# Routing stage of a convolution, mixture-of-experts and attention kernel: one product for centred channels and logits, choices marked on GpSimd, keys in one pass

## The chip, the cores and the metric

The kernel runs on one core of one Trainium2 chip. The metric is the time of one execution on the device in microseconds. The kernel before was run ten times: median 9578.8 us, from 9575.91 to 9595.06.

A core has five engines that this document names as the profile does: PE (matrix products; PEld is its weight load), DVE (vector operations), ACT (activation functions and scaled copies), POOL (GpSimd; it also issues the indirect transfers) and SP (issues most plain transfers). Each takes its own instructions in the order in which they were built and waits for the others by semaphores.

## The reference, cut to what matters

The input `x` is 32 images of 128 channels, 56 x 56. A layer of convolution with a mixture of experts is followed by a layer of attention with a second mixture; all is float32. The change lies in the routing of the first layer. There are T = 100352 tokens (one for each pixel), C = 128 channels, E = 8 experts, two choices a token:

```python
x = conv(input, dw_kernel) + dw_bias            # depthwise 7 x 7
mu = x.mean(-1); var = x.var(-1)
x = (x - mu) / sqrt(var + 1e-06) * ln_gamma + ln_beta
logits = x @ Wg + bg
topv, topi = top_k(logits, 2)
wts = softmax(topv)
order = argsort(-wts[:, 0])                     # tokens by their first weight
cap = int(1.25 * T / E)                         # places of an expert, filled in this order
```

A choice counts only while its expert has a place left. The kept tokens go through the experts and their weighted results come back to the tokens.

## The kernel before, in words

The kernel runs in stages, one after the other, over tiles of 128 partitions:

- **Convolution** (to about 700 us): 128 channels, one after the other; the result goes to `conv_d` in memory.
- **Route** (L323 to L393): the tokens in NG = 112 groups of 896, a group being GJ = 7 tiles of 128 tokens. `route(g)` is a generator whose `yield`s mark its steps; `in_turn` (L179) takes one step of each group under way in turn, so that several groups interleave. The scheduler then fixes the order on each engine.
- **Selection** (L397 to L654): for each expert, the tokens' keys, and by 24 halvings the threshold above which tokens are kept.
- **Scatter** (L659 to L808): group by group, the places of the kept tokens are worked out and their rows sent to the experts' buffer `xb_d` by indirect transfers.
- **Experts**, **attention** (from L926) and the **second mixture and output** follow; the change does not touch them.

`route(g)` in steps, with its lines:

1. L358: SP loads the group's channels into `ct` (four buffers, from pool `rt`).
2. L364: PE multiplies each of the seven tiles by `jm` (128 wide), which gives the centred channels (with the sign turned) in PSUM tiles `pc` of four tiles' width, four buffers of one bank. ACT squares them: four tiles singly with a running sum (L372), three in one go (L367), whose sums DVE makes (L368). L377: PE multiplies the same seven tiles by the 8 columns of `rw` that hold the routing weights; the logits before scaling are in `pl`, two buffers. A float32 product is two instructions of PE in the trace.
3. `inverse` (L139): ACT makes mean square plus eps, logarithm and exponential (L143 to L145), then POOL makes one Newton step in four operations (L147 to L150). The result is 1/sqrt(var), in `rst`.
4. DVE scales the logits by it (L381) and adds their constant part `cb` (L382); they are in `lgs`.
5. DVE finds the eight largest of each tile's logits (L387, seven MAX8) and their indices (L389, seven FIND_INDEX8, each with a load of values). ACT copies the first two of both into `pk` (L390, L391), a tile of four numbers a token.

After all groups, the selection begins at L405: from the two largest logits come `ex`, `den`, `share` and the priority `prio` (L405 to L413). Then for each expert e the key (L417 to L423): two DVE passes compare the two index columns of `pk` with e, a third multiplies by `prio`, and ACT subtracts a constant. One pass is over 784 numbers in each of 128 partitions.

In the scatter, `places(g)` (L749) writes a group's seven row numbers a partition into `rd`, which has the pool's four buffers; `send(g)` (L796) issues seven indirect transfers on POOL from them (L697). The rows themselves are in six tiles `xs`.

Of the kernel before, what the change touches and what calls it, by code (L numbers as in the profile page):

```python
# [8 lines left out]
F32 = mybir.dt.float32  # L9
I32 = mybir.dt.int32  # L10
U32 = mybir.dt.uint32
AF = mybir.ActivationFunctionType
ALU = mybir.AluOpType
AX = mybir.AxisListType
# [3 lines left out]
P = 128  # L18
GJ = 7
# [6 lines left out]
def conv_attn_hybrid_kernel(  # L26
# [24 lines left out]
    nc = tc.nc  # L51
    N, C, H, W = x.shape
    HW = H * W
    T = N * HW
    E = Wg.shape[1]
# [19 lines left out]
    TC = T // P  # L75
# [43 lines left out]
    def over(t, n):  # L119
        return t.unsqueeze(2).to_broadcast([t.shape[0], t.shape[1], n])  # L120

    def across(t, n):
        return t.unsqueeze(1).to_broadcast([t.shape[0], n, t.shape[1]])
# [12 lines left out]
    def by_tile(t):  # L136
        return t.rearrange("c (j p) -> c j p", p=P)
# [61 lines left out]
    with tc.tile_pool(name="cv_c", bufs=1) as cc, tc.tile_pool(  # L199
        name="cv", bufs=3  # L200
# [20 lines left out]
        for c in range(C):  # L221
# [15 lines left out]
            for kw in range(KS):  # L237
                for r in range(2):
                    rows = slice(r * HP, r * HP + H)
                    for b in range(2):  # L240
# [4 lines left out]
                            start=(kw == 0),  # L245
                            stop=(kw == KS - 1),
# [18 lines left out]
    CHUNKS = ((0, 4), (4, GJ))  # L265
# [5 lines left out]
    rst = ch.tile([P, TC], F32, name="rst")  # L271
# [38 lines left out]
    count = ch.tile([P, P // E], F32, name="count")  # L310
# [7 lines left out]
    rw = ch.tile([C, RO], F32, name="rw")  # L318
    cb = ch.tile([P, C + E], F32, name="cb")

    pairs = ExitStack()
    pk = pairs.enter_context(tc.tile_pool(name="pairs", bufs=1)).tile([P, TC, 4], F32, name="pk")
    with tc.tile_pool(name="rt_c", bufs=1) as cc, tc.tile_pool(  # L323
        name="rt", bufs=4
    ) as rt, tc.tile_pool(name="rt_p", bufs=2, space=PSUM) as rtp:
        tc.keep_in_program_order(
            nc.scalar.preload_act_table_set("natural_log_exp_and_others")
        )
        gam = cc.tile([C, 1], F32, name="gam")
        nc.sync.dma_start(gam, ln_gamma.unsqueeze(1))  # L330
        nc.sync.dma_start(bet, ln_beta.unsqueeze(1))
        wg = cc.tile([C, E], F32, name="wg")
        nc.sync.dma_start(wg, Wg)
        bgt = cc.tile([P, E], F32, name="bgt")
        nc.sync.dma_start(bgt, bg.partition_broadcast(P))

        jm = cc.tile([C, C], F32, name="jm")
        nc.vector.tensor_scalar(jm, ident, 1.0 / C, None, ALU.subtract)
        raw = cc.tile([C, RO], F32, name="raw")
        nc.vector.tensor_copy(raw[:, :C], ident)  # L340
        nc.vector.tensor_copy(raw[:, C : C + C], turn)
        nc.vector.tensor_copy(raw[:, C + C :], wg)

        ps = rtp.tile([P, RO], F32, name="pa", bufs=1)
        nc.tensor.matmul(ps, bet.to_broadcast([C, P]), raw, start=True, stop=True)
        nc.vector.tensor_copy(cb[:, :C], ps[:, :C])
        nc.vector.tensor_tensor(cb[:, C:], ps[:, C + C :], bgt, ALU.add)
        nc.vector.tensor_scalar(raw, raw, gam, None, ALU.mult)
        ps = rtp.tile([P, RO], F32, name="pa", bufs=1)
        nc.tensor.matmul(ps, jm, raw, start=True, stop=True)  # L350
        nc.vector.tensor_copy(rw, ps)

        def route(g):
            pr, gl = divmod(g, GPP)
            cols = slice(g * GJ, (g + 1) * GJ)
            ct = rt.tile([C, GT], F32, name="ct")
            for im, px, col, n in segments(gl):
                nc.sync.dma_start(ct[:, col : col + n], conv_d[2 * pr + im, :, px : px + n])  # L358
            yield
            ss = rt.tile([P, GJ], F32, name="ss")  # L360
            for i, (j0, j1) in enumerate(CHUNKS):
                ps = rtp.tile([P, 4, C], F32, name="pc", bufs=4)
                for j in range(j0, j1):
                    nc.tensor.matmul(ps[:, j - j0, :], by_tile(ct)[:, j, :], jm, start=True, stop=True)  # L364
                if i:
                    sq = rt.tile([P, GJ - 4, C], F32, name="sqs", bufs=2)
                    nc.scalar.activation(sq, ps[:, : j1 - j0, :], AF.Square)  # L367
                    nc.vector.tensor_reduce(ss[:, j0:j1], sq, AX.X, ALU.add)  # L368
                else:
                    for j in range(j0, j1):  # L370
                        sq = rt.tile([P, C], F32, name="sq", bufs=2)
                        nc.scalar.activation(  # L372
                            sq, ps[:, j - j0, :], AF.Square, accum_out=ss[:, j : j + 1]
                        )
            pl = rtp.tile([P, GJ, E], F32, name="pl")
            for j in range(GJ):
                nc.tensor.matmul(pl[:, j, :], by_tile(ct)[:, j, :], rw[:, C + C :], start=True, stop=True)  # L377
            yield
            yield from inverse(rt, ss, 0, "rst", 3, rst[:, cols])
            lg = lgs[:, cols, :]  # L380
            nc.vector.tensor_tensor(lg, pl, over(rst[:, cols], E), ALU.mult)  # L381
            nc.vector.tensor_tensor(lg, lg, across(cb[:, C:], GJ), ALU.add)  # L382
            yield
            m8 = rt.tile([P, GJ, 8], F32, name="m8")
            i8 = rt.tile([P, GJ, 8], U32, name="i8")
            for j in range(GJ):
                nc.vector.max(m8[:, j, :], lg[:, j, :])  # L387
            for j in range(GJ):
                nc.vector.max_index(i8[:, j, :], m8[:, j, :], lg[:, j, :])  # L389
            nc.scalar.copy(pk[:, cols, 0:2], m8[:, :, 0:2])  # L390
            nc.scalar.copy(pk[:, cols, 2:4], i8[:, :, 0:2])  # L391

        in_turn(route(g) for g in range(NG))  # L393

    with tc.tile_pool(name="sel", bufs=1) as se, tc.tile_pool(  # L397
        name="sel2", bufs=2
# [1 line left out]


        HALF = 2.0**23
        ea = [pk[:, :, 2], pk[:, :, 3]]
        ex = se.tile([P, TC], F32, name="ex")
        nc.vector.tensor_tensor(ex, pk[:, :, 1], pk[:, :, 0], ALU.subtract)  # L405
        nc.scalar.activation(ex, ex, AF.Exp)
# [4 lines left out]
        prio = se.tile([P, TC], F32, name="prio")  # L411
# [3 lines left out]
        nc.vector.memset(less, -HALF)  # L415
        key = se.tile([P, E, TC], F32, name="key")
        for e in range(E):  # L417
            nc.vector.tensor_scalar(key[:, e, :], ea[0], float(e), None, ALU.is_equal)
            nc.vector.scalar_tensor_tensor(
                key[:, e, :], ea[1], float(e), key[:, e, :], ALU.is_equal, ALU.add  # L420
            )
            nc.vector.tensor_tensor(key[:, e, :], key[:, e, :], prio, ALU.mult)
            nc.scalar.activation(key[:, e, :], key[:, e, :], AF.Identity, bias=less)  # L423

        def total(cnt):
# [233 lines left out]
    with tc.tile_pool(name="sc_c", bufs=1) as cc, tc.tile_pool(  # L659
        name="sc", bufs=4  # L660
# [88 lines left out]
        def places(g):  # L749

            of = ofs.pop(g)
            ve.tensor_tensor(of, of, nexts.pop(g), ALU.mult)
            at_ = sc.tile([P, GJ], F32, name="at", bufs=2)
            ve.tensor_reduce(at_, of, AX.X, ALU.add)
            rds[g] = sc.tile([P, GJ], I32, name="rd")
            ve.tensor_scalar(rds[g], at_, float(ROWS), None, ALU.add)

        def add_beta(g):
# [772 lines left out]
```

## Time and profile before

| | us |
|---|---|
| median of 10 runs | 9578.8 |
| lowest and highest | 9575.91 and 9595.06 |
| the profiled execution | 9579.57 |
| its span | 9577.9 |

Busy time in its span, and in the stages as the table of windows gives them:

| window, us | what runs there | PE | DVE | ACT | POOL | granted clock |
|---|---|---|---|---|---|---|
| whole span | | 8677.5 | 6478.3 | 5266.4 | 6773.6 | 0.942 |
| 0 to 700 | convolution | 684.15 | 132.28 | 83.56 | 3.73 | 1.00 |
| 700 to 1063 | route | 356.69 | 274.65 | 247.28 | 94.45 | 0.98 |
| 1063 to 1098 | keys | 0.00 | 34.66 | 9.27 | 3.39 | 0.50 |
| 1098 to 1315 | thresholds, sizes | 57.81 | 169.33 | 110.78 | 19.03 | 0.60 |
| 1315 to 2340 | scatter | 786.94 | 832.06 | 374.26 | 775.22 | 0.93 |
| 2340 to 4430 | experts | 1950.50 | 494.70 | 712.93 | 1623.97 | 0.98 |
| 4430 to 9000 | attention | 4325.30 | 4376.55 | 3712.33 | 4253.83 | 0.98 |
| 9000 to 9578 | second mixture, output | 516.14 | 164.12 | 15.97 | 0.00 | 0.57 |

How to read it: the stages follow each other, so the engine that bounds one of them is seen only in its own row. The granted clock is the share of full speed at which PE may run. A group of instructions is printed as line, engine, operation, tiles written and read, sizes, count, then busy us, mean ns of one, and the idle time before them with what ended it. A tile's name stands without its buffer number, and a line of a helper stands for all that call it (L161 is that of the class which keeps an order of the text).

### The profile page before, as it was taken

What the parts mean: (1) busy time and instruction counts of PE and PEld (TensorE: products, weight loads), DVE (VectorE), ACT (ScalarE), POOL (GpSimd) and SP (SyncE); (2) the same over time, 40 slices, a digit from 0 to 9 for tenths busy, and PEclk for the clock granted to TensorE, in tenths of its full rate; (3) what the DMA queues carried; (4) which work ended last, traced back from release to release, by engine and by line L of the source; (5) the groups of instructions that cost most, each with busy time, mean ns of one, the idle gap of its engine ahead of it and who ended that gap; (6) DMA issues with size and microseconds to landing.
All of it is one profiled execution on the core that took longest, in us unless ns stands there. A gap on an engine that the chain in (4) does not pass through costs nothing. (4 is left out here: it accounts for less than half of the span.)

```text
span 9577.9 us, 165805 instructions
## 1 busy us (share of the span) xinstructions
PE 8677.5 (91%) x62536; PEld 7131.6 (74%) x62536; DVE 6478.3 (68%) x10965; ACT 5266.4 (55%) x13385; POOL 6773.6 (71%) x4884
## 2 busy tenths in 40 slices
PE   9999467776999999997999999999999999999888
PEld 3569445555766666666888998998988898889853
DVE  2127888885222222226999999999999999999423
ACT  1117633333333333335888888888888888888400
POOL 0002147776777777787999999999999999999300
PEclk9999789998999999999999999999999999999765
DMA  9995247775444444441000000000000000000389
GB/s 209 213 200 147 59 124 211 209 207 157 70 70 63 65 68 70 69 69 32 24 31 31 31 31 30 25 27 31 31 31 31 31 24 31 31 31 26 98 279 331
DMA packets 1019570, 849.94 MB, mean 89 GB/s; under 512 B 525876, under 2 KB 912247, under 8 KB 999250
## 3 DMA queue, kind: packets, MB, share of 16 engines
q1 hardware_dynamic: 464018, 479.57, 18.0%
q0 software_dynamic: 177664, 188.81, 11.2%
q10 hardware_dynamic: 377088, 170.96, 6.7%
q8 instruction: 495, 8.11, 0.4%
q14 instruction: 305, 2.50, 0.1%
HBM read 486.34 MB, written 353.64 MB: 88 GB/s over the span
## 5 line engine op out<-in xcount | busy, mean ns | idle before, releaser
L161 POOL TENSOR_TENSOR s<-s,q 128x2048 f32<-128x2048 f32 x784 | 3597.5, 4599 | 137.8 <-DVE s L161 104.5
L161 ACT ACTIVATE s<-s 128x2048 f32<-128x2048 f32 x784 | 1500.6, 1914 | 686.3 <-POOL s L161 683.6
L161 POOL DMA_INDIRECT t_d<-ys,xe x992 | 1530.5, 1543 | 417.1 <-issue 229.9
L161 DVE TENSOR_TENSOR s<-kv,c 128x2048 f32<-128x2048 f32 x784 | 1788.4, 2281 | 7.9 <-POOL c L161 7.6
L161 DVE TENSOR_TENSOR ev<-s,kv 128x2048 f32<-128x2048 f32 x784 | 1785.7, 2278 | 2.3 <-ACT s L161 2.2
L161 PE MATMUL sm<-ident,ev 128*128 128x128 f32 x12544 | 1532.5, 276 | 45.9 <-DVE ev L161 45.9
L161 PE MATMUL sm<-ident,s 128*128 128x128 f32 x12544 | 1524.9, 275 | 8.0 <-ACT s L161 8.0
L161 PEld LDWEIGHTS sm<-ident,ev 128*128 128x128 f32 x12544 | 1437.6, 144 | 93.6 <-DVE ev L161 51.3
L161 PEld LDWEIGHTS sm<-ident,s 128*128 128x128 f32 x12544 | 1402.9, 143 | 20.5 <-ACT s L161 8.4
L888 ACT ACTIVATE hT<-ph,b1t 128x512 f32<-128x512 f32 (+1 forms) x992 | 679.6, 685 | 1239.5 <-PE ph L884 1224.0
L899 DVE TENSOR_TENSOR ys<-py,b2t 128x512 f32<-128x512 f32 (+1 forms) x248 | 171.5, 691 | 1536.1 <-PE py L894 1439.3
L894 PEld LDWEIGHTS py<-w,hT 128*128 128x128 f32 x7936 | 961.1, 193 | 202.5 <-issue 92.2
L884 PE MATMUL ph<-xeT,w 128*128 128x512 f32 (+1 forms) x1984 | 923.3, 598 | 70.6 <-DVE xeT L880 70.6
L894 PE MATMUL py<-w,hT 128*128 128x128 f32 x7936 | 985.1, 278 | 0.2
L697 POOL DMA_INDIRECT xb_d<-xs,rd x784 | 766.6, 978 | 240.2 <-issue 199.2
L241 PE MATMUL cps<-xin,br 56*64 56x448 f32 x7168 | 684.2, 539 | 12.8 <-DVE br L235 10.6
L884 PEld LDWEIGHTS ph<-xeT,w 128*128 128x128 f32 x1984 | 348.7, 191 | 393.8 <-issue 294.1
L161 PE MATMUL pa<-rw,ct 128*128 128x256 f32 x1568 | 422.5, 414 | 203.2 <-DVE xs L161 203.2
L241 PEld LDWEIGHTS cps<-xin,br 56*64 56x64 f32 x7168 | 345.2, 132 | 350.9 <-issue 310.7
L161 PEld LDWEIGHTS pa<-rw,ct 128*128 128x128 f32 x1568 | 299.8, 203 | 335.8 <-DVE xs L161 248.0
L287 POOL MEMSET code<- 128x64 f32 x1 | 0.2, 152 | 693.2 <-DMA conv_d<-ot 693.2
L161 PE MATMUL kv<-wq,zT 128*128 128x256 f32 x1568 | 416.8, 389 | 54.6 <-DVE ev L161 54.2
(327 smaller groups left out, 13452.3 us busy)
## 6 DMA issues: line engine op xcount, KB each, us to landing
ct<-conv_d SPq DMA_DIRECT2D x192, 448.0 KB
xin<-in_x_dram SPq DMA_DIRECT2D x256, 196.0 KB
conv_d<-ot ACTq DMA_DIRECT2D x512, 98.0 KB
t_d<-xs ACTq DMA_DIRECT2D x112, 448.0 KB
tr<-t_d SPq DMA_DIRECT2D x112, 448.0 KB
to<-t_d SPq DMA_DIRECT2D x32, 1568.0 KB
out_dram<-oo ACTq DMA_DIRECT2D x32, 1568.0 KB
xg<-in_x_dram SPq DMA_DIRECT2D x96, 448.0 KB
```

Source lines behind the costliest of these rows:

```text
L161: r = getattr(self.engine, name)(*a, **k)
L241: nc.tensor.matmul(pss[r][b * HP : (b + 1) * HP], br[rows, kw, :], xi[rows, b * NB : (b + 1) * NB, kw : kw + W], start=(kw == 0), stop=(kw ...
L287: nc.gpsimd.memset(code, -1.0)
L697: s = nc.gpsimd.indirect_dma_start(out=xb_d, out_offset=bass.IndirectOffsetOnAxis(ap=idx, axis=0), in_=row, in_offset=None, bounds_check=R ...
L884: nc.tensor.matmul(ph[:, :, :rows], w1[:, f * P : (f + 1) * P], xT[:, :, :rows], start=True, stop=True,)
L888: nc.scalar.activation(hT[:, f, :, :rows], ph[:, :, :rows], AF.Gelu, bias=b1t[:, f : f + 1])
L894: nc.tensor.matmul(py[:rows, j, :], hT[:, f, j, :rows], w2[:, f, :], start=(f == 0), stop=(f == NF - 1),)
L899: nc.vector.tensor_tensor(ys[:rows], py[:rows], across(b2t, SB)[:rows], ALU.add)
```

## The change

Route:

- `jl` holds `jm` and the 8 columns of the routing weights side by side, 136 columns, and one product a tile gives both the centred channels and the logits. The seven tiles of a group lie in PSUM as `pc`, two banks with three tiles each and two buffers, and `po`, one tile, two buffers.
- Of the squares, tiles 0 to 2 and 6 are taken singly and tiles 3 to 5 in one go.
- The logits are scaled from `pc` in one DVE operation of six tiles and from `po` in a second. The constant part is added by POOL instead of DVE.
- The two largest logits are copied to `pk`, now two numbers a token; the two indices go to `ei`. POOL subtracts both from the numbers 0 to 7 (`off`), and the product of the two differences, zero for the two experts that were chosen, is in `hot`.

Selection: a key is one DVE pass, `hot` equal to zero times `prio`, and the same ACT operation behind it.

Scatter: `rd` has eight buffers in place of four.

```diff
-    pk = pairs.enter_context(tc.tile_pool(name="pairs", bufs=1)).tile([P, TC, 4], F32, name="pk")
+    pa_ = pairs.enter_context(tc.tile_pool(name="pairs", bufs=1))
+    pk = pa_.tile([P, TC, 2], F32, name="pk")
+    hot = pa_.tile([P, TC, E], F32, name="hot")
...
+        CE = C + E
+        jl = cc.tile([C, CE], F32, name="jl")
+        nc.vector.tensor_copy(jl[:, :C], jm)
+        nc.vector.tensor_copy(jl[:, C:], rw[:, C + C :])
+        JH = GJ // 2
...
-            for i, (j0, j1) in enumerate(CHUNKS):
-                ps = rtp.tile([P, 4, C], F32, name="pc", bufs=4)
-                for j in range(j0, j1):
-                    nc.tensor.matmul(ps[:, j - j0, :], by_tile(ct)[:, j, :], jm, start=True, stop=True)
-                if i:
-                    sq = rt.tile([P, GJ - 4, C], F32, name="sqs", bufs=2)
-                    nc.scalar.activation(sq, ps[:, : j1 - j0, :], AF.Square)
-                    nc.vector.tensor_reduce(ss[:, j0:j1], sq, AX.X, ALU.add)
...
-            pl = rtp.tile([P, GJ, E], F32, name="pl")
+            pc = rtp.tile([P, 2, 512], F32, name="pc")
+            po = rtp.tile([P, CE], F32, name="po")
+            at_ = pc[:, :, : JH * CE].rearrange("p i (j c) -> p i j c", c=CE)
             for j in range(GJ):
-                nc.tensor.matmul(pl[:, j, :], by_tile(ct)[:, j, :], rw[:, C + C :], start=True, stop=True)
+                nc.tensor.matmul(
+                    po if j == 2 * JH else at_[:, j // JH, j % JH, :], by_tile(ct)[:, j, :], jl,
+                    start=True, stop=True,
+                )
+            for j in (*range(JH), 2 * JH):
+                sq = rt.tile([P, C], F32, name="sq", bufs=2)
+                nc.scalar.activation(
+                    sq, po[:, :C] if j == 2 * JH else at_[:, 0, j, :C], AF.Square,
+                    accum_out=ss[:, j : j + 1],
+                )
+            sq = rt.tile([P, JH, C], F32, name="sqs", bufs=2)
+            nc.scalar.activation(sq, at_[:, 1, :, :C], AF.Square)
+            nc.vector.tensor_reduce(ss[:, JH : 2 * JH], sq, AX.X, ALU.add)
...
-            nc.vector.tensor_tensor(lg, pl, over(rst[:, cols], E), ALU.mult)
-            nc.vector.tensor_tensor(lg, lg, across(cb[:, C:], GJ), ALU.add)
+            r = rst[:, cols]
+            nc.vector.tensor_tensor(
+                lg[:, : 2 * JH].rearrange("p (i j) e -> p i j e", i=2), at_[:, :, :, C:],
+                r[:, : 2 * JH].rearrange("p (i j) -> p i j", i=2).unsqueeze(3).to_broadcast(
+                    [P, 2, JH, E]
+                ),
+                ALU.mult,
+            )
+            nc.vector.tensor_scalar(lg[:, 2 * JH], po[:, C:], r[:, 2 * JH :], None, ALU.mult)
+            nc.gpsimd.tensor_tensor(lg, lg, across(cb[:, C:], GJ), ALU.add)
...
-            nc.scalar.copy(pk[:, cols, 0:2], m8[:, :, 0:2])
-            nc.scalar.copy(pk[:, cols, 2:4], i8[:, :, 0:2])
+            nc.scalar.copy(pk[:, cols, :], m8[:, :, 0:2])
+            ei = rt.tile([P, GJ, 2], F32, name="ei")
+            nc.scalar.copy(ei, i8[:, :, 0:2])
+            yield
+            off = rt.tile([P, 2, GJ, E], F32, name="off_")
+            nc.gpsimd.tensor_tensor(
+                off, count[:, :E].unsqueeze(1).unsqueeze(1).to_broadcast([P, 2, GJ, E]),
+                ei.rearrange("p j i -> p i j").unsqueeze(3).to_broadcast([P, 2, GJ, E]),
+                ALU.subtract,
+            )
+            nc.gpsimd.tensor_tensor(hot[:, cols, :], off[:, 0], off[:, 1], ALU.mult)
...
-            nc.vector.tensor_scalar(key[:, e, :], ea[0], float(e), None, ALU.is_equal)
             nc.vector.scalar_tensor_tensor(
-                key[:, e, :], ea[1], float(e), key[:, e, :], ALU.is_equal, ALU.add
-            )
-            nc.vector.tensor_tensor(key[:, e, :], key[:, e, :], prio, ALU.mult)
+                key[:, e, :], hot[:, :, e], 0.0, prio, ALU.is_equal, ALU.mult
+            )
...
-            rds[g] = sc.tile([P, GJ], I32, name="rd")
+            rds[g] = sc.tile([P, GJ], I32, name="rd", bufs=8)
```

In the changed kernel the product is L374, the squares L380 and L385, the sums L386, the scaling L391 and L398, POOL's add L399, MAX8 and FIND_INDEX8 L404 and L406, the copies L407 and L409, `off` L412, `hot` L417, `ex` L430 and the key's pass L443.

More of the change, by code (lines that the diff above doesn't have):

```diff
@@ L351, in conv_attn_hybrid_kernel @@
         nc.vector.tensor_copy(rw, ps)
+        CE = C + E
[3 more added lines that the diff above has]
+        JH = GJ // 2
+        assert 2 * JH + 1 == GJ and JH * CE <= 512
         def route(g):
@@ L360, in route @@
             ss = rt.tile([P, GJ], F32, name="ss")
-            for i, (j0, j1) in enumerate(CHUNKS):
-                ps = rtp.tile([P, 4, C], F32, name="pc", bufs=4)
-                for j in range(j0, j1):
-                    nc.tensor.matmul(ps[:, j - j0, :], by_tile(ct)[:, j, :], jm, start=True, stop=True)
-                if i:
-                    sq = rt.tile([P, GJ - 4, C], F32, name="sqs", bufs=2)
-                    nc.scalar.activation(sq, ps[:, : j1 - j0, :], AF.Square)
-                    nc.vector.tensor_reduce(ss[:, j0:j1], sq, AX.X, ALU.add)
[L369 to L373, printed above, removed]
-                        )
-            pl = rtp.tile([P, GJ, E], F32, name="pl")
-            for j in range(GJ):
-                nc.tensor.matmul(pl[:, j, :], by_tile(ct)[:, j, :], rw[:, C + C :], start=True, stop=True)
+            pc = rtp.tile([P, 2, 512], F32, name="pc")
+            po = rtp.tile([P, CE], F32, name="po")
+            at_ = pc[:, :, : JH * CE].rearrange("p i (j c) -> p i j c", c=CE)
+            for j in range(GJ):
+                nc.tensor.matmul(
[11 more added lines that the diff above has]
+            nc.vector.tensor_reduce(ss[:, JH : 2 * JH], sq, AX.X, ALU.add)
             yield
@@ L402, in conv_attn_hybrid_kernel @@
         HALF = 2.0**23
-        ea = [pk[:, :, 2], pk[:, :, 3]]
         ex = se.tile([P, TC], F32, name="ex")
```

## The prediction

> **What bounds the kernel now.** I read the table of windows first, then the waits, the time line of one group, and the groups by line. Route lasts from 702.7 us to 1063.4 us, where L405 begins the selection; the change acts there, in the selection's keys, and in one buffer count of the scatter. First the table of windows, for the middle of route and of the scatter (columns: window, its length, then busy us and instructions of PE, PEld, DVE, ACT and POOL, granted clock, DMA share, GB/s):
>
> ```profile
> 720.00:1050.00 330.00, 330.00 (x2955) 330.00 (x2955) 255.15 (x2523) 232.55 (x1479) 86.57 (x424) 1.00 0.51 147
> 1400.00:2250.00 850.00, 673.11 (x3063) 501.25 (x3062) 709.57 (x2290) 318.26 (x953) 648.00 (x664) 0.94 0.75 210
> ```
>
> In route PE never rests; DVE has 77%, ACT 70%, POOL 26%. A group takes 3.128 us: 28 matmul instructions (an fp32 product is two), 0.1117 us apart, wide or narrow alike; 112 groups make 350.3 us. The stage from its first product to L405 is 360.7 us, so fill and drain are 10.4 us. The waits of 720 to 1050 us (who waited, for whom, total us, times, longest) say that other engines wait for PE or for their own chain, never PE for them:
>
> ```profile
> POOL rst L147 <- ACT rst L145: 223.3, 106, 7.6
> ACT sqs L367 <- PE pc L364: 70.5, 100, 0.7
> DVE lgs L381 <- POOL rst L150: 3.3, 6, 1.8
> ```
>
> **PE's part.** The 14 narrow instructions of a group go. The other 14 become 136 wide. The distance between instructions at 256 columns (L161 pa, 0.21 us) is twice that at 128, so 136 cost about 0.115 us: 1.6 us a group instead of 3.13. PE stops being the bound; the question is what is.
>
> **What the engines need.** DVE loses L382 (0.25 us from start to start) and gains a small scaling, 0.13: 2.42 (77.4% of 3.128) becomes 2.30 us. ACT stays at 2.2 us. POOL gains three operations. None is in the trace; nearest rows:
>
> ```profile
> L161 POOL TENSOR_TENSOR kx<-kx 128x16 f32<-128x16 f32 x392 | 88.8, 226 | 30.1 <-DVE kx L161 30.1
> L161 POOL TENSOR_TENSOR c<-q,kx 128x128 f32<-128x128 f32 x112 | 42.7, 402 | 4.4
> L524 POOL TENSOR_TENSOR kept<-kept,eq 128x784 f32<-128x784 f32 x8 | 18.5, 2312 | 199.2 <-DVE eq L523 199.2
> ```
>
> Between the first two, 1.6 ns an element: the add and `hot` of 56 elements 0.285 us, `off` of 112 0.375. The third row's 2.7 ns an element would make them 0.33 and 0.48; the 7-element row (0.20) is the lower end. POOL: 1.14 + 0.285 + 0.375 + 0.285 = 2.1 us. Were throughput all, a group would take 2.3 us.
>
> The Trainium skill's page "GPSIMD Engine Reference", section 4.1, speaks against this part: elementwise work with two inputs belongs on VectorE. By the 2.6 cycles of 1.2 GHz an element of its section 3.1 an estimate of add and `off` is 0.31 and 0.43 us; what follows would grow by about 6 us in all.
>
> **The order decides.** Every engine takes its instructions in the built order, and in the changed program these chains stand in each other's way. The built order goes in turns of two groups. With a, b two groups and c, d the next two:
> - DVE: scale a; seven MAX8 and seven FIND_INDEX8 of a; scale b; MAX8, FIND_INDEX8 of b; sums of c, of d; scale c.
> - POOL: add a, root of b, `off` a, add b, `hot` a, `off` b, `hot` b, root of c, add c.
> - ACT: copies of a, squares of c, copies of b, two squares of d, L143 of c, a square, L144, a square, L145, squares of d, root of d.
> - PE: products of c wait for scale a, of d for scale b, because a product's bank is now held until its logits are scaled and there are two.
>
> So b's add stands on POOL behind `off` a, which waits for ACT's index copy of a, which waits for a's FIND_INDEX8; b's MAX8 wait for that add. The root of c waits on ACT behind the index copy of b. Before, the add was DVE's own next instruction, no POOL operation waited for a choice, and `pc` had twice the banks. The pieces have durations in this time line of before (start, us, instruction):
>
> ```profile
> 902.49 0.28 ACT L372 ACTIVATE sq<-pc 128x128 f32<-128x128 f32 x1 [0.21 <-PE pc L364]
> ...
> 903.07 0.58 DVE L387 MAX8 m<-lgs 128x8 f32<-128x8 f32 x7
> ...
> 903.79 0.22 ACT L145 ACTIVATE rst<-rst 128x7 f32<-128x7 f32 x1
> 904.09 0.20 POOL L147 TENSOR_TENSOR rst<-rst 128x7 f32<-128x7 f32 x1 [2.06 <-ACT rst L145]
> ...
> 904.44 0.16 DVE L389 FIND_INDEX8 i<-m,lgs 128x8 uint32<-128x8 f32 x1
> ...
> 904.95 0.20 POOL L150 TENSOR_TENSOR rst<-rst 128x7 f32<-128x7 f32 x1
> ```
>
> ACT's eleven records from the first of two squares to the end of L145 take 1.52 us, and from there to the end of L150 it is 1.14; both sequences stand in the changed order too. MAX8 and FIND_INDEX8 of a group take 1.52 (903.07 to 904.60). A signal costs 0.03 us between DVE and ACT and 0.08 to POOL (904.01 to 904.09).
>
> One turn, from the end of L150 of a to that of c: scale a with its remainder 0.32; signal and add a 0.36; MAX8 and FIND_INDEX8 of a 1.55; index copy 0.24; signal and `off` 0.45; rest of add b 0.22; MAX8 and FIND_INDEX8 of b 1.55; index copy and the step to the squares 0.18; squares and root on ACT 1.54; root on POOL 1.14. Sum **7.55 us for two groups** where PE took 6.26. The products lie beside it: c's 1.6 us end some 0.5 us before the squares need them, d's likewise. With the ends of POOL's prices (three operations on the chain) the turn is 7.2 to 7.8. SP's loads of `ct` land 3.4 us after issue, with four buffers, so some 12 us ahead: never late.
>
> **The clock.** In a turn PE now works about 3.3 us of 7.55, and rests 3.7 us in one piece. From the trace's clock records beside its matmul starts: in the scatter the grant changes in steps of 3.41 us; it fell to half after steps in which PE issued for less than 0.42 of the time and came back after steps above 0.80. 0.44 on average is at that edge, so the grant will alternate. At half clock fourteen instructions take 3.1 us instead of 1.56, as before shows just after route's start:
>
> ```profile
> 713.76 3.00 PE L377 MATMUL pl<-rw,ct 128*128 128x8 f32 x14
> 716.61 3.33 PE L364 MATMUL pc<-jm,ct 128*128 128x128 f32 x14
> ```
>
> Then the products join the chain: thirteen of c and d to the squares of d 5.55, latency 0.3, squares and root 1.54, POOL's root 1.14, scaling c and signals 0.35, near 9.0 us. PE then works 6.2 of 9.0, so full grants return. I take 8.1 us, a good third of the way. Route: 56 x 8.1 + 5 of fill and drain (most of the drain is now part of a turn; in the 5 is that the first product waits for `jl`, and L430 for the last `hot`, behind POOL's `negl` of 1.57) = 458.6 us, **+98** against 360.7. All full: 56 x 7.55 + 5 = 428, +67. All half: 509, +148.
>
> The Trainium skill's page "TensorE: Matmul & The Clock Gate", Part 1, has the clock fall after an idle window of about 3.4 us. The rows above show falls after windows that were up to 0.42 busy. By the page's rule a rest of 3.7 us would rarely hold a whole window, the clock would stay full, and the time would be that of the all-full case.
>
> **Keys.** Before, from L405 (1063.35) to the last product of a key (1097.01): 33.7 us, three DVE passes for each of eight experts. After: one pass each, but all wait for `prio`, so nothing fills DVE while Exp runs: L405 2.10, Exp with signals 1.06, den 0.56, reciprocal 5.0, two limits 1.1, eight passes at 1.46 (L419, which also reads a strided tile, 1.53 long) 11.7: 21.5. **-12.2 us.** Ends: 1.03 (L514, unstrided) and 2.10 (L405, strided twice) a pass: -15.6 to -7.
>
> **Eight buffers for the places.** The wait that goes, DVE's `rd` for the row transfers (69.7 us, 46 times in the scatter window), is DVE waiting for POOL's queue. POOL issues 784 transfers 1.275 us apart, 648 of 850 us busy and the rest its own 0.30 us between them; 1004 us in all, the scatter's whole length. DVE will run ahead to the six row buffers instead and wait there. Nothing, within -3 to +3; if POOL had rests, the most is the 7.6 us it waited for those transfers.
>
> **Sum.** The profiled execution took 9579.57 us around a span of 9577.9, 0.8 above the median of 9578.8. 9579.6 + 98 - 12 + 0 = 9665.
>
> **Rivals.**
> 1. The same chain, clock full throughout: +67 - 12, 9634. For it: half clock costs PE its rest and so restores the grant. Against: 0.44.
> 2. The same chain, clock half nearly throughout: +148 - 12, 9715. Against: at half, steps above 0.80 occur.
> 3. Faster: the chains interleave over several turns and DVE becomes the bound, 112 x 2.30 + 10 = 268, -93 - 12, 9475. It decides where a turn falls below 6.47 us (6.26 + 12/56), that is if index copy, `off` and b's add (0.91) and 0.2 more left the chain. For it: POOL waits most of route and has room. Against: the built order, which puts them there.
> 4. Chain shorter than I make it by 1 us: near 9590, no change.
>
> **Chances.** Forecast 0.58, rival 1 0.18, rival 2 0.12, rival 3 0.08, rival 4 0.04. The range reaches over rivals 1 and 2 with the short ends of POOL and keys: 9620 to 9722. Slower by over 0.2% (about what a measurement can tell from no change) 0.88, within 0.04, faster 0.08.
>
> **What would show it.** Route from its first product to `ex` near 458 us; PE's starts in pairs of groups 8 us apart, with a rest over 3 us; clock 0.6 to 0.8 there; ACT waiting for DVE's index finds, DVE's MAX8 for POOL's add, PE for DVE's scaling; no engine above 70% busy. `ex` to the last key pass 21 us. The scatter's POOL records 1.275 us apart as before. It is wrong if DVE is over 90% busy in route, or if PE has no rests in pairs.

## The result, and the profile after

The changed kernel takes **9657.3 us** (median of 8 runs, 9654.25 to 9663.71) where the kernel before takes 9579.05 on the same chip: ratio **1.0081**, 95% interval 1.0072 to 1.0090. It is 78 us slower. The forecast was 9665, in a range from 9620 to 9722.

By stages, from the two profiled executions (spans 9577.9 and 9657.9):

| stretch, us | before | after | difference | forecast |
|---|---|---|---|---|
| start to the route's first product | 702.7 | 709.5 | +6.8 | not priced |
| first product to `ex` (route) | 360.7 | 452.2 | +91.5 | +98 |
| `ex` to the last key out of ACT | 34.7 | 21.7 | -13.0 | -12.2 |
| from there to the end | 8479.8 | 8474.6 | -5.2 | 0 |

The last row is not the change's: over all profiled executions of this study that stretch lies between 8469 and 8481.

The table of windows, for the middle of route and, moved by 90 us, for the middle of the scatter (window, length, then busy us and instructions of PE, PEld, DVE, ACT and POOL, granted clock, DMA share, GB/s):

```profile
720.00:1050.00 330.00, 196.45 (x1169) 184.14 (x1167) 193.77 (x1991) 196.94 (x1162) 147.40 (x578) 0.85 0.40 116
1490.00:2340.00 850.00, 659.72 (x3135) 481.77 (x3134) 733.84 (x2350) 328.23 (x980) 648.45 (x662) 0.99 0.76 214
```

In route no engine is above 60% now, where PE had 100%. A stage in which all engines are half idle is set by a chain of waits, and the waits of 720 to 1050 us name its links (who waited, for whom, total us, times, longest):

```profile
PE pc L374 <- ACT rst L143: 94.9, 30, 3.6
DVE ss L386 <- ACT sqs L385: 77.7, 54, 3.0
ACT ei L409 <- DVE i L406: 51.2, 69, 0.8
DVE m L404 <- POOL lgs L399: 48.8, 83, 0.8
```

Before, PE waited for nobody. Now it rests up to 3.6 us in one piece, DVE's MAX8 wait for POOL's add, and ACT for the indices. The first row needs care: it names ACT, because that signal came last by the profile. What the products need of the earlier group is DVE's scaling, and the time line of one turn shows that PE starts 0.1 us behind its end (start, us, instruction; here a turn at full clock):

```profile
956.65 0.20 POOL L150 TENSOR_TENSOR rst<-rst 128x7 f32<-128x7 f32 x1
956.88 0.21 DVE L391 TENSOR_TENSOR lgs<-pc,rst 128x48 f32<-128x48 f32 x1 [0.23 <-POOL rst L150]
957.19 1.63 PE L374 MATMUL pc<-jl,ct 128*128 128x136 f32 x12 [2.89 <-ACT rst L143]
957.31 0.30 POOL L399 TENSOR_TENSOR lgs<-lgs,cb 128x56 f32<-128x56 f32 x1 [0.46 <-DVE lgs L398]
957.64 0.57 DVE L404 MAX8 m<-lgs 128x8 f32<-128x8 f32 x7 [0.42 <-POOL lgs L399]
...
958.66 0.40 PE L374 MATMUL po<-jl,ct 128*128 128x136 f32 x2
...
959.21 0.20 ACT L409 CAST ei<-i 128x14 f32<-128x14 uint32 x1 [0.75 <-DVE i L406]
...
959.49 0.39 POOL L412 TENSOR_TENSOR off__9303<-count,ei 128x112 f32<-128x112 f32 x1 [0.80 <-ACT ei L409]
...
959.83 0.31 POOL L399 TENSOR_TENSOR lgs<-lgs,cb 128x56 f32<-128x56 f32 x1
...
960.17 0.58 DVE L404 MAX8 m<-lgs 128x8 f32<-128x8 f32 x7 [0.76 <-POOL lgs L399]
...
960.84 0.40 PE L374 MATMUL po<-jl,ct 128*128 128x136 f32 x2
...
961.73 0.20 ACT L409 CAST ei<-i 128x14 f32<-128x14 uint32 x1 [0.75 <-DVE i L406]
961.84 0.27 ACT L380 ACTIVATE sq<-pc 128x128 f32<-128x128 f32 x1
...
963.43 0.21 POOL L147 TENSOR_TENSOR rst<-rst 128x7 f32<-128x7 f32 x1 [0.66 <-ACT rst L145]
...
964.32 0.20 POOL L150 TENSOR_TENSOR rst<-rst 128x7 f32<-128x7 f32 x1
```

From one end of L150 (956.85) to the next of the same place in the pattern (964.52) is 7.67 us for two groups, and each line begins when the work of the one before it in the chain is done (a group's seven FIND_INDEX8 lie between its MAX8 and the copy of L409). The chain is the one that the prediction wrote down, link by link.

PE is no link of this turn. The products of the first of the next two groups end at 959.06 us (958.66 and 0.40), and its squares, which stand on ACT behind the index copy of 959.21, start at 959.31, 0.25 later. Those of the second end at 961.24, 0.60 before its squares at 961.84. At full clock the links on DVE, ACT and POOL alone add up to the 7.67 us.

The clock: PE's own time line shows three turns, 8.19, 8.03 and 7.67 us from start to start (940.97, 949.16, 957.19, 964.86), and the pattern repeats.

```profile
940.97 1.77 PE L374 MATMUL pc<-jl,ct 128*128 128x136 f32 x12 [3.62 <-ACT rst L143]
...
943.15 2.89 PE L374 MATMUL pc<-jl,ct 128*128 128x136 f32 x12
...
949.16 3.06 PE L374 MATMUL pc<-jl,ct 128*128 128x136 f32 x12 [2.90 <-issue]
...
957.19 1.63 PE L374 MATMUL pc<-jl,ct 128*128 128x136 f32 x12 [2.89 <-ACT rst L143]
```

Twelve instructions take 1.63 us at full clock and 3.06 at half. In two of these three turns a part of the products runs slowed; the mean of the three is 7.96.

The grant changes in steps of 3.41 us. The table of windows, cut at these steps, shows what decides (columns as above; PE's busy time is the first after the length, the granted clock the third from the end):

```profile
938.90:942.32 3.41, 1.35 (x11) 1.38 (x12) 1.79 (x16) 1.86 (x11) 1.82 (x9) 1.00 0.29 117
942.32:945.73 3.41, 3.41 (x16) 3.16 (x15) 2.66 (x33) 1.98 (x12) 1.05 (x4) 0.50 0.42 117
...
952.56:955.97 3.41, 1.74 (x15) 1.54 (x14) 1.66 (x18) 3.23 (x22) 0.89 (x3) 1.00 0.55 143
955.97:959.38 3.41, 1.87 (x15) 1.73 (x15) 2.63 (x26) 1.21 (x7) 1.76 (x9) 1.00 0.38 126
```

After a step in which PE was busy for 1.35 of 3.41 us, 0.40, the next one has half clock; after one of 1.74, 0.51, the clock stays full. From 730 to 1150 us the grant fell 34 times, each time after a step with a share from 0.16 to 0.40; it stayed full after 54 steps with shares from 0.42 to 0.67; and every step at half clock, being 0.82 busy or more, was followed by a full one. So half clock lasts one step at a time.

Three more readings. The start: the first small product waits 9.7 us, behind the tokens' loads (groups by line, 690 to 712 us).

```profile
L347 PE MATMUL pa<-raw,bet 128*128 128x264 f32 x2 | 1.2, 712 | 9.7 <-DMA ct<-conv_d 9.7
```

Before, that product stood behind the first groups' products on PE; now `jl` comes from it, so the first group waits too. SP issues the load of `bet` behind four loads of tokens, at 699.73 us. The keys (groups by line, 1160 to 1190 us of after):

```profile
L443 DVE SCALAR_TENSOR_TENSOR key<-hot,prio 128x784 f32<-128x784 f32 x8 | 11.9, 1555 | 0.0
...
L430 DVE TENSOR_TENSOR ex<-pk 128x784 f32<-128x784 f32 x1 | 1.0, 976 | 1.1 <-POOL hot L417 1.1
```

And the scatter: POOL's transfers stay back to back (980 ns each where they were 978), the 784 of them take 1006.0 us from first to last start where they took 1004.1. The wait that the eight buffers took away has a successor, in the waits of 1490 to 2340 us:

```profile
DVE xs L161 <- DMA xb_d<-xs,rd: 50.7, 63, 3.3
```

The row `DVE rd`, 69.7 us before, is gone; DVE stands at the six row tiles instead.

### The profile page after: what moved, and what is told of

Same layout as the page of the kernel before. It is cut to its first block, busy times and chain, and to the rows that moved or that the text cites. A ratio compares the mean times of both kernels' runs of the same rounds, so it can differ in the third digit from the quotient of the medians.

```text
span 9657.9 us, 163304 instructions
## 1 busy us (share of the span) xinstructions
PE 8562.3 (89%) x60968; PEld 6931.0 (72%) x60968; DVE 6462.5 (67%) x10951; ACT 5290.5 (55%) x13385; POOL 6885.7 (71%) x5220
## 5 line engine op out<-in xcount | busy, mean ns | idle before, releaser
L241 PEld LDWEIGHTS cps<-xin,br 56*64 56x64 f32 x7168 | 283.4, 132 | 411.6 <-issue 410.6
L161 PE MATMUL pa<-rw,ct 128*128 128x256 f32 x1568 | 395.1, 392 | 139.8 <-DVE xs L161 139.4
```

Source lines behind the costliest of these rows:

```text
L161: r = getattr(self.engine, name)(*a, **k)
L241: nc.tensor.matmul(pss[r][b * HP : (b + 1) * HP], br[rows, kw, :], xi[rows, b * NB : (b + 1) * NB, kw : kw + W], start=(kw == 0), stop=(kw ...
```

## The experiments

Two theories about the 452 us. **H, the held bank:** a group's products wait for the scaling two groups earlier, because the logits now stay in the bank until the root is there. **O, the order on the engines:** it is the place of the add, the marks and the index copy in the queues of POOL, ACT and DVE that makes the turn. "Route" below is always the length from the first product to `ex` in the run's profiled execution. A rerun of the changed route (the early beta column, below) gave 452.6 after 452.2, so differences of some us are readable there (the route of before varies by more, up to 369.1, as told under the parts beside the route); the ratios are to the kernel before on the same chip.

### The add back on DVE, and the marks taken out

```diff
-            nc.gpsimd.tensor_tensor(lg, lg, across(cb[:, C:], GJ), ALU.add)
+            nc.vector.tensor_tensor(lg, lg, across(cb[:, C:], GJ), ALU.add)
```

> The adding of cb goes back from POOL to DVE; products, marks, keys and buffers as after. Theory O, by the sum of the prediction: adding a 0.36, the index copy 0.24, the marks' first pass 0.45 and the rest of adding b 0.22 leave the turn, two adds of about 0.14 on DVE come in, 1.27 - 0.28 = 1.0 us less a turn, 56 turns: about 9600 (9590 to 9615). Theory H: the held bank and the clock carry the turn, the other links have work beside them; at most a part of it shows: 9640 to 9670.

Measured: 9639.7 us, ratio 1.0060 (1.0041 to 1.0079); route 426.8, granted clock 0.91. 25 us off the route, half of what O wanted and more than H's middle; the total stands at H's lower edge.

The other one takes `off` and `hot` out of the loop and brings the keys of before back:

```diff
-            yield
-            off = rt.tile([P, 2, GJ, E], F32, name="off_")
...
-            nc.gpsimd.tensor_tensor(hot[:, cols, :], off[:, 0], off[:, 1], ALU.mult)
```

> No marks on POOL: the two passes, the index copy's own tile and the one-pass keys go, four numbers a token and three-pass keys come back as before; one product, the add on POOL and two banks as after. The keys give back 13.0 us (33.66 against 20.71 from the start of ex to the last key pass). Theory O: 0.45 and 0.24 leave each turn, 39 us less, 9657 - 39 + 13 = 9631 (9620 to 9640). Theory H: nothing of the turn is saved, 9657 + 13 = 9670 (9660 to 9682).

Measured: 9659.9 us, ratio 1.0079 (1.0058 to 1.0100); route 434.3, clock 0.89. The route gives 18 us, the keys take 13 back. 18 is between the two theories (0 and 39), and the total stands just under H's range.

### The one product alone

Both edits together, so that of the route's change only the joint product, its banks and the two scalings are left:

> The one product alone: no marks on POOL, keys in three passes, the add on DVE as before; two banks that wait for the scaling. Singly, the add on DVE took 25.4 us off the route (452.2 to 426.8) and the marks 17.8 (to 434.3). Theory H: the turn still goes from bank to bank through squares, root and scaling, and the two links add up at most: route 405 to 427, total 9657 - 47 to 25 + 13 = 9623 to 9645, still slower than before by 0.5%. Theory O: without the orders on POOL nothing holds the turn above the engines' work, the route falls below before's 361 and the total to 9579 or less.

Measured: 9643.2 us, ratio 1.0068 (1.0053 to 1.0084); route 418.5, within H's 405 to 427. O falls in the form expected here: with nothing of the change left on POOL, the route is still 58 us longer than before. H is not shown by it: DVE and ACT still have the orders of after (the second group's scaling behind the first one's FIND_INDEX8, the index copy ahead of the squares), and O, as it is stated for the third buffer below, names these too. Its PE time line (same columns as above):

```profile
1004.44 1.63 PE L373 MATMUL pc<-jl,ct 128*128 128x136 f32 x12 [3.13 <-ACT rst L143]
...
1011.48 1.75 PE L373 MATMUL pc<-jl,ct 128*128 128x136 f32 x12 [3.13 <-ACT rst L143]
```

Still two groups a turn, still a rest of 3.1 us, and 7.04 us from start to start. The four routes make a square:

| route, us | add on DVE | add on POOL |
|---|---|---|
| no marks | 418.5 | 434.3 |
| marks on POOL | 426.8 | 452.2 |

The add alone costs 15.8, the marks alone 8.3, both 33.7, 9.6 more than their sum: only with both does the add of one group stand behind the marks of another. The turns at full clock say the same by themselves: 7.04 us with neither, 7.30 with the add on POOL, 7.06 with the marks, 7.67 with both. So the marks alone hardly lengthen a full turn; their 8.3 us lie in the other turns, of about 7.35 and 8.0 us, of which that run has more.

### The bank: a third buffer, and an early copy out of it

```diff
-            pc = rtp.tile([P, 2, 512], F32, name="pc")
-            po = rtp.tile([P, CE], F32, name="po")
+            pc = rtp.tile([P, 2, 512], F32, name="pc", bufs=3)
+            po = rest[:, g % 3, :]
```

(`rest` is one shared tile of three slots, made once.)

> Three buffers in place of two for the products' banks (the last product of each group goes into one shared bank, so that eight banks suffice); all else as after. Theory H, the held bank: PE's start of a group waits for the scaling two groups earlier, because logits now stay in the bank until the root is there; a chain of 7.96 us per two groups then carries three groups, 5.3 us per two or 2.65 a group, 112 groups 297 us in place of 452; since POOL and ACT then stand closer to each other I allow up to 346. Total 9657 - 106 to 155 = 9502 to 9551. Rival theory O, the order of the engines' queues (the add behind the marks on POOL, the scaling of b behind MAX8 and FIND of a on DVE, the index copy behind the squares on ACT): another bank changes none of these, and the turn stays above 7 us: over 9605.

Measured: 9555.6 us, ratio **0.9972** (0.9963 to 0.9982), faster than before; route 341.8, inside the 297 to 346 that H gave it, though the total is 5 us above H's range. A part of it is its own make: the shared tile brings a new wait, as the waits of 760 to 1040 us show.

```profile
PE rest L376 <- DVE lgs L400: 15.7, 48, 0.3
```

The second way keeps two buffers and lets ACT copy the raw logits out behind the squares; DVE then scales in SBUF (the lines of the scaling out of the bank go):

```diff
+            lg = lgs[:, cols, :]
+            nc.scalar.copy(
+                lg[:, : 2 * JH].rearrange("p (i j) e -> p i j e", i=2), at_[:, :, :, C:]
+            )
+            nc.scalar.copy(lg[:, 2 * JH], po[:, C:])
             nc.vector.tensor_reduce(ss[:, JH : 2 * JH], sq, AX.X, ALU.add)
...
+            nc.vector.tensor_tensor(lg, lg, over(rst[:, cols], E), ALU.mult)
```

> As after, with two banks, but ACT copies the raw logits out of the banks right behind the squares, and DVE scales them in their rows in SBUF; the add stays on POOL and the marks stay. Theory H: the bank is free once the squares and two short copies are done and no longer waits for the root; then no engine waits for the bank for long and the busiest sets the pace, DVE 2.3 or ACT 1.6 + two copies of some 0.3 each, 2.3 to 2.6 us a group, 258 to 291 us and about 5 at the end in place of 452: 9463 to 9501. Theory O: the same queue orders stand, the turn stays above 7 us: over 9605; anything between tells that both have a share.

Measured: 9521.8 us, ratio **0.9935** (0.9913 to 0.9956); route 302.8, clock 1.00 from 760 to 960 us. The route is 149 us shorter than after by two small copies a group, and what PE waits for are those copies, at most 1.1 us at a time (waits of 760 to 1040 us):

```profile
PE pc L374 <- ACT lgs L387: 71.8, 97, 1.1
```

It is 7 us above H's upper end, 2.63 us a group; the total is 21 above, of which some is the execution: in the profiled one the convolution ended 14 us later than in after.

One thing neither theory had foreseen. Rival O took the engines' orders as given, whatever the banks. They were not: in the time lines of both kernels the groups no longer go in pairs: POOL has one root, one add and one group's marks in each round, where after has two of each. The two buffers had put the groups in pairs in the built order too. So "bank" and "order of pairs" went together in these two runs, and their shares are not told apart; what is shown is that freeing the bank removes both. The turn of after shown above speaks for the order: there PE had 0.25 and 0.60 us to spare, so a turn at full clock would not have become shorter by a free bank with the orders left as they are.

### The clock, by itself

Six more products into a spare bank behind every second group, read by nobody (extra work, nothing left out):

```diff
+            if g % 2:
+                spare = rtp.tile([P, CE], F32, name="spare", bufs=1)
+                for j in range(6):
+                    nc.tensor.matmul(spare, by_tile(ct)[:, j, :], jl, start=True, stop=True)
```

> After, with six more products into a spare bank behind every second group, which nothing reads: extra work for PE in its wait, so that the granted clock does not fall. If the clock (0.85 from 720 to 1050 us) is a part of the loss as the prediction has it, it goes to 0.95 or more and the turn to 7.55 (the prediction's sum) to 7.67 (two groups at full clock in the trace of after): 56 turns and 5 us, 428 to 435 in place of 452: 9633 to 9641. If the clock has no part in it, no change, or the extra products (6 x about 0.45 us, 2.7 a turn, against a wait of about 3) delay the next group: 9657 to 9700.

Measured: 9648.9 us, ratio 1.0073 (1.0058 to 1.0089); route 442.0, clock 0.94.

```profile
760.00:1040.00 280.00, 198.68 (x1442) 187.07 (x1441) 166.87 (x1729) 170.55 (x1008) 127.49 (x505) 0.94 0.40 120
```

The clock rose, though not to 1, and the route fell by 10 us with more work in it: a part of the loss was the clock's. The expected 17 to 24 would have needed the full grant; most turns here are 7.66 us, some still 8.0 to 8.2. The total lies between the two ranges that were expected, and is not separated from that of after by its interval; the route's length is.

> The add back on DVE and the six spare products together: the price of the add on POOL at full clock. Theory O, the prediction's sum: the turn falls by 1.0 from what the six products alone give, 56 us less. Theory H: the add's place and the clock were partly the same saving (with the add on DVE alone the clock rose from 0.85 to 0.91); 20 to 40 us less than with the six products alone: 9595 to 9620.

Measured: 9623.4 us, ratio 1.0046 (1.0031 to 1.0062); route 411.3, 30.7 less than with the six products alone, as H expected and not O's 56; clock 0.97 from 760 to 960 us. Its full-clock turn is 7.05 us against 7.66. **So the add on POOL is worth 0.6 us a turn, not the 1.0 of the prediction's links.** DVE's time line of this run says why:

```profile
1002.13 0.16 DVE L410 FIND_INDEX8 i<-m,lgs 128x8 uint32<-128x8 f32 x1
1002.21 0.19 DVE L395 TENSOR_TENSOR lgs<-pc,rst 128x48 f32<-128x48 f32 x1
1002.32 0.21 DVE L402 TENSOR_SCALAR lgs<-po,rst 128x8 f32<-128x8 f32 x1
1002.56 0.22 DVE L403 TENSOR_TENSOR lgs<-lgs,cb 128x56 f32<-128x56 f32 x1
1002.82 0.51 DVE L408 MAX8 m<-lgs 128x8 f32<-128x8 f32 x6
```

From the end of a's last FIND_INDEX8 (1002.29) to b's first MAX8 it is 0.53 us, because b's scaling and add now stand there themselves; with the add on POOL, in the run with the six products alone, it is 0.99. The rest is the same stretch for a, from the root's end to MAX8: 0.66 for 0.79.

### The parts beside the route

> The kernel before, with POOL's marks and the one-pass keys alone: separate products, four banks, DVE's add as before. Theory H: PE is busy for the whole route before (330.0 of 330.0 us), POOL 0.26, and two POOL passes of 0.39 and 0.30 a group fit in; the route stays 361, the keys give 13.0: 9579 - 13 = 9566 (9562 to 9572). Rival: POOL and DVE hinder each other, or the root's passes on POOL queue behind the marks and PE waits; 0.1 us a group would be 11 us and eat the gain: 9575 to 9585.

The edit is the marks and the one-pass keys of the change, on the kernel before. Measured: 9566.6 us, ratio 0.9990 (0.9981 to 0.9999); from `ex` to the last key 21.7 where it was 34.7. Where PE is the bound, the marks cost nothing that is seen. Its route is 367.0, 6 longer than the profiled one of before, but so is that of the next run, which has before's route: in both the clock is 0.55 to 0.68 from 720 to 740 us, where the profiled execution of before shows 0.99.

```diff
-            rds[g] = sc.tile([P, GJ], I32, name="rd")
+            rds[g] = sc.tile([P, GJ], I32, name="rd", bufs=8)
```

> The kernel before with eight buffers for the rows' places and nothing else. The prediction: 0 (3 either way), POOL's row transfers stay back to back, 9576 to 9583, the scatter's length 1016.6 as before. Rival: the places' two buffers held the scatter up: it shortens by more than 5 us and the total falls below 9574.

Measured: 9583.4 us, ratio 1.0004 (0.9995 to 1.0014); 784 transfers in 1005.8 us (1004.1 before). The wait moves to the row tiles as in after (`DVE xs` for the transfers, 58.6 us). No difference.

```diff
+        bet0 = cc.tile([C, 1], F32, name="bet0")
+        nc.sync.dma_start(bet0, ln_beta.unsqueeze(1))
...
-        nc.tensor.matmul(ps, bet.to_broadcast([C, P]), raw, start=True, stop=True)
+        nc.tensor.matmul(ps, bet0.to_broadcast([C, P]), raw, start=True, stop=True)
```

> After, with a second load of the beta column ahead of the convolution for the small product; nothing else. If the first product stands 6.8 us later than before because that load is issued behind the tokens' loads, it comes back to about 703 and the total to 9650 (9645 to 9655), the route's length unchanged at 452. If something else held it (the weights' own chain of four small steps, 4.0 us from the first small product to the group's first): 2 to 3 us only, 9653 to 9656.

Measured: 9654.4 us, ratio 1.0079 (1.0063 to 1.0094). The first product is back at 702.1 us (709.5 in after), the route 452.6. The start is shown to come from that load. The total was 3 lower, less than the runs can tell; the remainder of the kernel was 6 us longer in this profiled execution.

### The version that the runs point to

Early copy on ACT, scaling and add on DVE, early load of beta, marks and one-pass keys kept:

> ACT copies the raw logits out early, DVE scales and adds in SBUF, marks and one-pass keys stay, two banks, and a second load of the beta column ahead of the convolution for the small products at the start. Worked from the run with the early copy and POOL's add (route 302.8 us, 2.63 a group from place to place): DVE's busy share there was 226 of 280 us, 2.12 a group, and takes on the add's 0.14; ACT 230 of 280, 2.16. Theory H, the bank no longer decides: 2.35 to 2.63 a group, route 268 to 300; first product back at about 703 as before (709.5 after): 703 + 268 to 300 + 22 + 8476, and 1 to 2 outside the span: 9470 to 9502, faster than both kernels. Rival: DVE is the fuller engine and the add costs it more than POOL's handing over did: 9505 to 9520.

Measured: **9496.9 us, ratio 0.9912** (0.9899 to 0.9926), 84 us faster than before and 160 faster than the change. Route 293.0. The first product came at 714.3 us and not at 703 in the profiled execution, whose convolution ended 11 us later than in after; in that of the next run it came at 703.4. From 740 to 940 us:

```profile
740.00:940.00 200.00, 148.97 (x1107) 133.04 (x1105) 194.47 (x1895) 179.76 (x1264) 116.12 (x474) 1.00 0.61 183
```

DVE is busy for 194.5 of 200 us: the route has a bounding engine again, and the clock is full. The rival was right that DVE is the fuller engine and wrong that this costs more than POOL's handing over.

> The same with three buffers of the products' banks. With the early copy and two, PE waited 71.8 of 280 us for ACT's copies. Theory H: that wait is only PE being the emptiest engine, the pace is DVE's and ACT's, and a third buffer changes nothing: within 5 us of the same kernel with two. If the bank still holds the pace: 0.1 to 0.2 us less a group, 11 to 22 us less.

Measured: 9494.1 us, ratio 0.9912 (0.9897 to 0.9927); route 292.8. No difference: PE's waits for ACT's copies (51.6 us of 200 with two buffers, 49.8 with three) are the rest of an engine that isn't the bound. With the early copy, the bank no longer holds anything up.

## Why the prediction was right, and where not

- **What bounds the change: right.** The chain, link for link. Measured on the turn shown above: scale and add of the first group, a, 0.79 us (forecast 0.68), MAX8 and FIND_INDEX8 of a 1.57 (1.55), index copy and signal 0.28, `off` and the add of the second group, b, 0.68 (together 0.96; forecast 0.24, 0.45 and 0.22, 0.91), MAX8 and FIND_INDEX8 of b 1.56 (1.55), step to the squares 0.11 (0.18), squares and root on ACT 1.52 (1.54), root on POOL 1.16 (1.14): 7.67 for 7.55. The bank stands beside this chain and not in it, as the prediction had it ("The products lie beside it", by some 0.5 us; measured 0.25 and 0.60); that the two banks go with the order in pairs was shown only by the runs that freed them.
- **POOL's prices from neighbouring rows: right.** 303 ns for 56 elements (forecast 285), 388 for 112 (375). The estimate made from the Trainium skill's page "GPSIMD Engine Reference" (section 3.1), 0.31 and 0.43, is 2% and 11% above these rows.
- **The clock: right that it falls and at which shares, too dark by how much.** "I take 8.1 us, a good third of the way" was 7.96; the granted clock was 0.85, not 0.6 to 0.8. Above the full-clock turn the clock costs 0.3 us a turn, 17 us in all, where 31 were taken. The 8.1 were a mix of turns of 7.55 and of about 9.0. But from 730 us on every step at half clock was busy enough to be the last, so no turn ran at half throughout: after the first two (8.4 and 9.3 us) none was longer than 8.2. That the mean came so near is in part luck. The rule of the page "TensorE: Matmul & The Clock Gate" (Part 1) as the prediction applied it would have left the clock full; this trace shows 0.85, and falls after steps in which PE was busy for up to 0.40.
- **Route +98: it was +91.5.** 56 turns of 7.96 are 446, and 6.4 are fill and drain (5 were taken).
- **The start: not priced.** The prediction knew that the first product waits for `jl`, put that into the 5 of fill and drain, and did not look at when `bet` is issued. It was 6.8 us, ahead of the stretch that it summed. So the close total is in part luck, two misses that cancel: 6.5 too much in the route, 6.8 too little ahead of it.
- **Keys -12.2: -13.0.** A pass over `hot` was 1.555 us (1.46 taken), L430 0.98 (2.10 taken): with two numbers a token in `pk` it costs what an unstrided pass cost before (979 ns).
- **Eight buffers 0: right,** and DVE waits where it was said to wait.
- **Rival 3's condition: wrong.** "It decides where a turn falls below 6.47 us, that is if index copy, `off` and b's add (0.91) and 0.2 more left the chain". With one product alone the 0.91 were out of the chain, and the turn at full clock fell by 0.63, to 7.04: links that leave a queue are replaced by what stood behind them, here b's scaling and add on DVE. What comes near to rival 3's case (DVE the bound, 9475; measured 9496.9) is the early copy, which frees the bank and with it the order in pairs. The prediction named the bank, last of its four engines, as "a product's bank is now held until its logits are scaled and there are two", and priced no way out of it.

## What to carry to other kernels

When one product is made to give two results, ask how long the bank stays taken: until the later reader of the two. Here the logits' reader stood behind a root that is made from the other result, and one early copy of 56 numbers a partition, with the other order of the groups that came with it, took 149 us off a route of 452. And a link on a measured chain is not worth its length: what waits behind it on the same engine moves up, so the gain is known only by taking it out.

## What the runs showed of the hardware that was not expected

**The clock went with PE's emptiest steps of 3.41 us, not with its share of work in the mean.** From 760 to 960 us (PE's busy share there, with the longest wait of the products from 760 to 1040 us):

| kernel | PE busy | longest wait, us | granted clock |
|---|---|---|---|
| after | 0.59 | 3.6 | 0.86 |
| marks taken out | 0.59 | 3.3 | 0.88 |
| add back on DVE | 0.57 | 3.4 | 0.91 |
| one product alone | 0.56 | 3.1 | 0.93 |
| six spare products | 0.71 | 2.2 | 0.94 |
| third buffer | 0.71 | 2.2 | 0.93 |
| six spare products, add on DVE | 0.74 | 1.9 | 0.97 |
| early copy | 0.72 | 1.1 | 1.00 |
| the version that the runs point to | 0.75 | 1.0 | 1.00 |

The third buffer and the early copy have the same share, 0.71 and 0.72, and a clock of 0.93 and 1.00. (A slowed product counts as busy for longer, so the shares of the slowed ones are flattered.) The longest wait goes with the clock better, but not strictly: 3.3 us stand beside 0.88 and 3.4 beside 0.91.

What holds in all of them is the reading by steps given for after. In the seven routes in which the clock fell, from 730 us to near the route's end, all 134 falls came after a step in which PE was busy for 0.44 or less; all 520 steps after which the clock stayed full had 0.42 or more; and every step at half clock had 0.82 or more and was followed by a full one. With the early copy and in the last version no stretch of that length between 760 and 960 us has less than 0.55, and the clock did not fall. By these numbers, as an estimate, a rest must cover about 2 us of one step (3.41 x 0.58) to bring the clock down. These are bounds for this route and no more.

At the route's start they do not hold. In the kernel before the grant fell at 713.6 us after a step in which PE was busy throughout, and in its run with eight buffers alone it stayed at half from 714.0 to 737.9 us with PE busy in every step.

**A strided read of two operands.** `ex` from `pk`: 2.10 us with 16 bytes from number to number, 0.98 with 8.

**Before's route is not always 361 us.** The same code took 369.1 in another execution, with the clock at 0.55 from 720 to 740 us. What decides at the start whether the grant comes back at once stays open.
